# Second expert product by seven products of quarter blocks, in a two-layer attention and mixture-of-experts kernel

## The chip, the core and the metric

One Trainium2 chip, one core. The metric is device time in microseconds (us) of one execution, the median of several runs. Engines are called as in the profile: PE (matrix products), DVE (vector), ACT (scalar, activations), POOL (GpSimd), SP (the queue that issues most plain DMAs). On-chip memory is SBUF, PE writes its results to PSUM.

## The reference, cut to what matters

4096 tokens in all, as 4 x 1024 in layer 0 and 8 blocks of 512 here; width 256. Four stages follow each other, each with a residual and layer norms: a gated attention and a low-rank feed-forward (layer 0), a 16-head attention with relu weights (layer 1), and a mixture of 8 experts with expert choice (layer 1). The change is mostly in the last; its lines:

```python
def _L1_ffn_ref(x, Wg, W1, b1, W2, b2):
    n = b * l                                  # 4096
    k = min(max(int(n * C / e), 1), n)         # 1024 tokens for each of 8 experts
    S = jax.nn.sigmoid(xt @ Wg).T
    G, I = jax.lax.top_k(S, k)
    ex = xt[I]
    hid = gelu(einsum('ekh,ehf->ekf', ex, W1) + b1)              # 256 -> 1024
    out = (einsum('ekf,efh->ekh', hid, W2) + b2) * G[..., None]  # 1024 -> 256
    new_x = zeros_like(xt).at[I.reshape(-1)].add(out.reshape(-1, h))
# then x = x + layernorm(new_x)
```

Each expert takes the 1024 tokens that score highest for it, so a token may be in several experts or in none.

## The kernel before, in words

All products are in float32. Layer 0 takes the first 400 us or so, layer-1 attention the time to about 966 us, the rest is the mixture of experts.

**Layer-1 attention.** Scores, relu and weighted values of 16 heads run as one stream on PE (L1528, L1549), the relu split between ACT (L1705) and DVE (L1707). A planner written out in the kernel, the loop from L1665 on, keeps estimates of when each engine is free. Other work comes as `Part`s, each with its cost per engine, its needs and a condition `when`; `beside` lists those with PE work, `rest` those without. `next_piece` picks a part to put on PE between two groups of scores, `go_on` releases the others. Two limits, MOST and AT_LAST, say how much may be released; AT_LAST holds for the last half block of queries. When a block, a half or (at the end) a quarter of a block is done, `close` (L1291) follows: output projection (`project_tile`, PSUM tile `pt` or, for the last quarter, `pts`), residual y, norms, the rows for the gate (`hg`), its transposes (`tpg`) and the gate product (`pg`). For the last quarter these steps are `at_once` (L1408), written out in order: first half of the projection, the weighted values' last division, `go_on_down_to(1)` (which releases what the earlier quarter still has open), then the second half of the projection.

**Search and lists.** For each expert the threshold of the 1024 best scores is found by steps of compare (L1819), count and a small PE product (L1833). Then the list of its tokens is built (sort, rank, `places` L1960, `collect` L1976) and its rows are gathered by eight indirect DMAs of 128 rows on POOL's queue (`got`, L2000). Expert 0's search and list run ahead; those of the others are steps of an `agenda`, taken by `go_on_with_lists(u, time)` between pieces of expert work.

**Experts.** An expert has 1024 tokens in two halves q of 512 (u = 2e + q), each of 4 chunks of 128 rows. `turn` (L2162) transposes gathered rows on PE and copies them to xT. In experts 0 to 2 and 7, `feed_forward(u)` (L2270) runs the first product, eight blocks of 128 hidden columns by 512 tokens, with gelu on ACT, then `project_back(u)` (L2302), so that each half goes through both products before the next. In experts 3 to 6 the first product covers both halves at once in `feed_forward_by_seven` (L2220): the 2x2 block product is formed by seven products instead of eight (Winograd's form), from sums of weights (`weight_sums`, L2185, four POOL operations of 128x512 for an expert, row L2195) and sums of tokens (`token_sums`, DVE, L2202). Then `project_back` runs twice.

**Second product.** `project_back` takes the chunks one by one: 8 matmuls of 128x256 into a PSUM tile `py` (two buffers), then on DVE bias (L2326) and gate (L2327) into y, then on POOL's queue an indirect DMA that adds the rows of y to `acc_d` in DRAM (L2328, one per chunk). Two scatters of one expert touch different rows, but the build orders each scatter behind the landing of the one before; only for expert 6 (`beside_each_other`) is that taken out. In expert 7 the sums stay in SBUF: `accg` is gathered from `acc_d` after the last scatter of expert 6, the product is added to it (L2322), and statistics, norms and outputs are woven in by the table `beside_last` (`read_back`, `all_stats` L2041, `all_out`, `known` L2087, `chosen_*`). `fetch_last` issues eight gathers of x (`xg`) for it. Weights of expert e + 2 are loaded (`load_expert`, SP, two of 1 MB) at the end of expert e.

[...]

Of the kernel before, what the change touches and what calls it, by code (L numbers as in the profile page):

```python
# [19 lines left out]
P = 128  # L20
D = 256
# [53 lines left out]
def kernel(  # L75
# [1028 lines left out]
    with ExitStack() as st3:  # L1104
# [186 lines left out]
        def close(t, h, oT, tiles, at_end):  # L1291

            y = None

            def new_y():
                nonlocal y
                y = wk.tile([P, NJ, D], F32, tag="y", name="y", bufs=1)
                last_use["y"] = [] if at_end else [parts[5, i] for i in tiles]

# [108 lines left out]
            def at_once(by_weight, back, go_on_down_to):  # L1408
# [8 lines left out]
                    project_tile(pt, i, (0,))  # L1417
                by_weight()
                back()
                go_on_down_to(1)  # L1420
                for i, pt in pts:
                    project_tile(pt, i, (1,))

                idle, psum = (two_banks(name)[:, 0, :] for name in ("idle", "psum"))
                ones = wk.tile([P, P], F32, tag="parts", name="ones")
# [69 lines left out]
            for i in tiles[1::2]:  # L1495
# [8 lines left out]
                        tensor=0.53, scalar=0.59,  # L1504
                    )
                )
            outs[0].when = lambda: done(last_use["y"])
            parts[7, tiles[0]].when = lambda: done(last_use["hg"])
            turns[0].when = may_turn
            gates = Part(gate, [(turns[-1], 1)], tensor=0.65, vector=0.4)  # L1510
# [154 lines left out]
        while True:  # L1665
# [6 lines left out]
                break  # L1672
            at = pe[0]
            Part.now = at / 1.6
            n = max(len(waiting) + len(made) - LAG, 0)
            group_ends, piece = False, None
            if n:
                left = to_end(waiting[0]) + 1
                if left <= n + 1:
                    n, group_ends = left, True  # L1680
                piece = next_piece(1 if not group_ends and left - n <= 2 * STEP else 0)
                if piece is not None and piece.spaced:
                    if since < 1 and len(beside) < MANY:
                        piece = None
                    else:
                        since = -1
                since += 1
            longer = piece.tensor if piece is not None else 0.0
            scored = at + 0.19
            end = scored + 0.22 * len(made) + 0.1 + 0.432 * n + longer  # L1690
            most = MOST if made[0][0][4] == 1 else AT_LAST
            by = end + (0.0 if any(part.ready() and part.takes[1] for part in rest) else 0.5)
            early = 0
            for k, (unit, sc) in enumerate(made):
                scored = max(scored, banks.pop(0)) + 0.22
# [54 lines left out]
    with ExitStack() as st4:  # L1750
# [28 lines left out]

        weights = [load_expert(0), load_expert(1)]  # L1780

        each = keep.tile([P, P, NTILE], BF16, name="each")
        behind_exp = mybir.DependencyInfo(mybir.DependencyClass.Sync, mybir.DependencyReason.DATA)
        whole = nc.scalar.activation(each, count_p.unsqueeze(2).to_broadcast([P, P, NTILE]), AF.Copy, scale=-1.0 / P)
        tc.add_manual_dep(whole.ins, state["exp"].ins.name, behind_exp, reason="the last scores go ahead")

        whole_c = keep.tile([P, NC], F32, name="whole_c")
# [93 lines left out]
        def in_stored(half):  # L1881

            room = xs[ADDED - 1].rearrange("p j d -> p (j d)")[:, half * TB : (half + 1) * TB]
            return room.bitcast(BF16).rearrange("p (a b) -> p a b", b=QT)

        class List:

# [72 lines left out]
            def places(self, part):  # L1960
                js = slice(part * QT, (part + 1) * QT)
                if part < 2:
                    self.at[part] = wk.tile([P, P, QT], BF16, tag="at", name="at", bufs=2)
                else:
                    self.at[part] = in_stored(part - 2)
                nc.vector.tensor_tensor(
                    self.at[part],
                    self.lo[:, js].unsqueeze(1).to_broadcast([P, P, QT]),
                    each[:, :, js],
                    ALU.is_equal,  # L1970
                )

            def collect(self, part):
                for j in range(part * QT, (part + 1) * QT):
                    u = 32 * (j % 4)
                    nc.tensor.matmul(  # L1976
                        parts[u : u + 2 * NC, 0:P],
                        lhsT=self.pair[:, j, :, :].rearrange("p v c -> p (v c)"),
                        rhs=self.at[part][:, :, j - part * QT],
                        start=(j < 4),  # L1980
                        stop=(j >= NTILE - 4),
                    )
                if part == 3:
                    self.listed = wk.tile([P, P], BF16, tag="listed", name="listed")
                    nc.scalar.copy(self.listed, parts[:, 0:P])
# [173 lines left out]
        QPE = NC // NJ  # L2159
        xT = {}  # L2160

        def turn(u, c, half=None):  # L2162

            if c == 0 and not half:
                xT[u] = wk.tile([P, DC, TB], F32, tag="xT", name="xT")
            e, q = divmod(u, QPE)
            tiles = range(NJ) if half is None else range(half * NJ // 2, (half + 1) * NJ // 2)
            tp = ps.tile([P, NJ, P], F32, tag="mm", name="tp", bufs=5)
            for i in tiles:
                nc.tensor.transpose(tp[:, i, :], lists[e].got[q * NJ + i][:, c * P : (c + 1) * P], ident)  # L2170
                if u == 0 and c == 0 and i == 0:

                    keep_busy(first, 4)
            cols = slice(tiles[0] * P, (tiles[-1] + 1) * P)
            copy = nc.scalar.copy if by_seven(e) else nc.vector.tensor_copy
            copy(xT[u][:, c, cols], tp.rearrange("p j t -> p (j t)")[:, cols])  # L2176

        def by_seven(e):
# [25 lines left out]
        def turns_within(u):  # L2204

            e, q = divmod(u, QPE)
            if u == QPE * NE - 1:
                return {}
            turns = {c: (lambda c=c: turn(u + 1, c)) for c in range(DC)}
            if q == QPE - 1 and by_seven(e + 1):  # L2210
                both = [
                    turns[0], turns[1], lambda: turn(u + 2, 0), lambda: token_sums(e + 1, 0), lambda: turn(u + 2, 1),
                    *(lambda n=n: token_sums(e + 1, n) for n in (1, 2, 3)),
                ]
                return {0: both[0:1], 1: both[1:4], 2: both[4:]}
            if by_seven(e) and q == 0:
                return {}
            return {2: [turns[0], turns[1]]} if u == 1 else {1: [turns[0]], 2: [turns[1]]}

        def feed_forward_by_seven(e):  # L2220
# [18 lines left out]
            for f in range(HC):  # L2239
# [19 lines left out]
                product(d, s4, b22, False, True, f)  # L2259
                nc.vector.tensor_tensor(c12, u2, d, ALU.add)  # L2260
                gelu(1, f, c12)
                go_on_with_lists(QPE * e, 3.0)
            for q in range(QPE):
                if q == 0 and by_seven(e + 1):
                    weight_sums(e + 1, gelus[-1])
                if q == 0 and e == NE - 2:
                    fetch_last()
                project_back(QPE * e + q, hid[q])

        def feed_forward(u):  # L2270
            e, q = divmod(u, QPE)
            w1, w2 = weights[e]
            hid = wk.tile([P, FC, TB], F32, tag="hid", name="hid")

            n = TB if u else TB // 2
            for h in range(TB // n):
# [3 lines left out]
                for f in range(FC):  # L2280
# [13 lines left out]
                    )  # L2294
                    if u or h or f not in (FC - 5, FC - 4, FC - 3):
                        go_on_with_lists(u, 1.75 if u else 0.87)
                    aside(u, "f", f)
            if q == QPE - 1 and by_seven(e + 1):
                weight_sums(e + 1, gelu)
            project_back(u, hid)  # L2300

        def project_back(u, hid):  # L2302

# [2 lines left out]
            ahead = turns_within(u)  # L2306
            for i in range(NJ):
                k = q * NJ + i
                py = ps.tile([P, D], F32, tag="y", name="py")
                for f in range(FC):  # L2310
                    nc.tensor.matmul(  # L2311
                        py,
                        lhsT=hid[:, f, i * P : (i + 1) * P],
                        rhs=w2[:, f, :],
                        start=(f == 0),
                        stop=(f == FC - 1),
                    )
                for do in ahead.get(i, ()):
                    do()
                gates = lists[e].got[k][:, D + e : D + e + 1]  # L2320
                if e == NE - 1:
                    nc.vector.scalar_tensor_tensor(accg[:, k, :], py, gates, accg[:, k, :], ALU.mult, ALU.add)  # L2322
                    aside(u, "i", i)
                    continue
                y = wk.tile([P, D], F32, tag="y", name="y", bufs=7)
                nc.vector.tensor_tensor(y, py, mb2[:, e, :], ALU.add)  # L2326
                nc.vector.tensor_scalar(y, y, gates, None, ALU.mult)  # L2327
                scatter = nc.gpsimd.indirect_dma_start(  # L2328
                    out=acc_d[:, :],
                    out_offset=lists[e].at_chunk(k),  # L2330
                    in_=y,
                    in_offset=None,
                    bounds_check=NT - 1,
                    oob_is_err=True,
                    compute_op=ALU.add,
                )
                if e == NE - 2:

                    beside_each_other(scatter, summed)
                go_on_with_lists(u, 3.4 if by_seven(e) else 2.3)  # L2340

# [85 lines left out]
```

## Time and profile before

| what | us |
|---|---|
| median of 3 runs | 1468.24 (1467.99 to 1468.54) |
| profiled execution: its own time | 1469.22 |
| its span, first to last instruction | 1467.0 |
| PE busy | 1414.9 |
| DVE, ACT, POOL busy | 869.4, 738.2, 530.3 |

The profile shows one execution; busy times are sums over the span, and an average over stages with different limits. Expert 0 begins at about 994 us, expert 1 at 1055, expert 2 at 1117, experts 3 to 6 at 1178, 1234, 1290 and 1346, expert 7 at 1401. The costliest groups of the experts' stage: second product L2311 (1024 records, 228.6 us), first product L2285 (288 records, 114.8 us), scatters L2328 (56, 88.5 us), gathers L2000. The profile has two records for each matmul instruction of these float32 products. A row of a group reads: line, engine, operation, output and inputs with shapes, count, then busy time and the mean ns of one (which overlap on PE, so that mean times count is more than busy), then idle time before it and what ended it. A row of a time line reads: start, length, engine, line, operation, and in brackets the idle time before it with what ended it. A row of the table by stretches has the stretch, its length, busy time and count for PE, PE's weight loads (PEld), DVE, ACT and POOL, the granted PE clock as a share, the share of DMA engines busy, and GB/s.

### The profile page before, as it was taken

The page shows a single profiled execution, that of the slowest core. Times are in us where ns is not written, and L with a number is a line of the kernel's source. Part 1 is how long each engine was busy: PE and PEld are TensorE (multiplying, and loading weights), DVE is VectorE, ACT ScalarE, POOL GpSimd, SP SyncE. Part 2 cuts the span into 40 slices and gives each one's busy share as a digit, 9 for nine tenths or more (in the row PEclk, how much of TensorE's full clock was granted, in tenths as well). Part 3 has the DMA queues.
Part 4 walks back from the last instruction along what each step waited for, and adds up shares of the span by engine and source line. Part 5 has one row for each costly group of instructions (what it writes and reads, how often), then busy time and mean ns, then how long its engine had stood idle before and what let it go on. Part 6 is the DMA issues. An engine that isn't in the chain of part 4 may idle for free. (4 is left out here: it accounts for less than half of the span.)

```text
span 1467.0 us, 26441 instructions
## 1 busy us (share of the span) xinstructions
PE 1414.9 (96%) x10392; PEld 859.9 (59%) x10392; DVE 869.4 (59%) x2134; ACT 738.2 (50%) x1013; POOL 530.3 (36%) x662
## 2 busy tenths in 40 slices
PE   8999999999899999999999999849999999999997
PEld 4666666667544545544554447617666657757674
DVE  5457655566554637574766587785545766364346
ACT  4244454443368887887878788522221131231243
POOL 4123232223352314333334223413425325543655
PEclk9999999999999999999999999969999999999999
DMA  8400000001642373448145611151414223343364
GB/s 223 139 1 1 1 1 1 1 1 59 209 143 88 115 232 101 138 137 240 55 140 170 191 59 31 45 162 39 104 22 126 49 76 69 80 100 60 78 168 133
DMA packets 104853, 138.76 MB, mean 95 GB/s; under 512 B 25469, under 2 KB 64794, under 8 KB 104602
## 3 DMA queue, kind: packets, MB, share of 16 engines
q1 hardware_dynamic: 74512, 81.75, 17.9%
q0 software_dynamic: 30160, 55.32, 15.8%
q8 instruction: 81, 1.33, 0.4%
q14 instruction: 42, 0.34, 0.1%
q10 hardware_dynamic: 58, 0.01, 0.0%
HBM read 75.29 MB, written 61.51 MB: 93 GB/s over the span
## 5 line engine op out<-in xcount | busy, mean ns | idle before, releaser
L1705 ACT ACTIVATE w<-sc 128x1024 f32<-128x1024 f32 x394 | 378.9, 1024 | 61.4 <-PE sc L1528 60.9
L1549 PE MATMUL po<-w,vaug 128*17 128x256 f32 (+1 forms) x4608 | 255.9, 358 | 1.0 <-DVE turned L1607 0.6
L2311 PE MATMUL py<-w,hid 128*128 128x256 f32 x1024 | 228.6, 380 | 0.0
L2311 PEld LDWEIGHTS py<-w,hid 128*128 128x128 f32 x1024 | 191.9, 190 | 29.6 <-issue 4.2
L1707 DVE TENSOR_SCALAR w<-sc 128x1024 f32<-128x1024 f32 x118 | 143.7, 1221 | 79.1 <-PE sc L1528 76.0
L1549 PEld LDWEIGHTS po<-w,vaug 128*17 128x17 f32 x4608 | 116.4, 97 | 117.3 <-issue 48.4
L1528 PE MATMUL sc<-q,kT 64*128 64x512 f32 (+1 forms) x1152 | 170.8, 404 | 2.9 <-ACT w L1705 1.5
L2328 POOL DMA_INDIRECT acc_d<-y,idx x56 | 88.5, 1579 | 164.6 <-issue 36.4
L1528 PEld LDWEIGHTS sc<-q,kT 64*128 64x128 f32 x1152 | 90.0, 184 | 84.1 <-issue 45.5
L2292 ACT ACTIVATE hid<-ph,mb 128x512 f32<-128x512 f32 (+1 forms) x72 | 46.0, 638 | 159.3 <-PE ph L2285 133.4
L2285 PE MATMUL ph<-xT,w 128*128 128x512 f32 (+1 forms) x288 | 114.8, 552 | 0.3 <-DVE xT L2176 0.3
L2000 POOL DMA_INDIRECT got<-tok_d,idx x64 | 66.3, 1036 | 76.3 <-DVE idx L1990 34.1
L2285 PEld LDWEIGHTS ph<-xT,w 128*128 128x128 f32 x288 | 52.6, 190 | 52.1 <-issue 49.1
L371 POOL DMA_DIRECT2D kT<-k_d x32 | 23.4, 732 | 117.9 <-PE sc L1528 54.3
L722 PE MATMUL pg<-nT,wh 128*128 128x512 f32 x128 | 61.4, 612 | 1.5 <-ACT nT L661 1.5
L2326 DVE TENSOR_TENSOR y<-py,mb 128x256 f32<-128x256 f32 x56 | 23.5, 420 | 65.8 <-PE py L2311 53.7
L848 PE MATMUL py<-wo,oT 128*128 128x256 f32 x256 | 61.6, 384 | 0.0
L738 PE MATMUL pv<-wh,nT 128*128 128x512 f32 x128 | 59.7, 592 | 0.0
L848 PEld LDWEIGHTS py<-wo,oT 128*128 128x128 f32 x256 | 47.5, 190 | 17.6 <-issue 11.1
L746 ACT ACTIVATE v<-v 128x512 f32<-128x512 f32 x32 | 20.2, 630 | 62.7 <-DVE v L745 62.7
L586 POOL TENSOR_TENSOR x<-x,y 128x1024 f32<-128x1024 f32 x13 | 30.6, 2355 | 56.3 <-ACT y L575 56.3
L1137 POOL TENSOR_TENSOR rsb<-veb,mhalf 128x1 f32<-128x1 f32 x30 | 19.7, 657 | 83.9 <-DVE veb L1136 83.9
(345 smaller groups left out, 2355.2 us busy)
## 6 DMA issues: line engine op xcount, KB each, us to landing
q<-q_d POOLq DMA_DIRECT2D x16, 1024.0 KB, 6.0
kT<-k_d POOLq DMA_DIRECT2D x32, 512.0 KB, 8.4
w<-in_L_ffn_W_dram SPq DMA_DIRECT2D x16, 1024.0 KB
k_d<-parts SPq DMA_DIRECT2D x48, 256.0 KB
q_d<-parts SPq DMA_DIRECT2D x48, 256.0 KB
acc_d<-logits SPq DMA_DIRECT2D x8, 512.0 KB
tok_d<-hg SPq DMA_DIRECT2D x30, 128.0 KB
x<-in_L_attn_x_dram SPq DMA_DIRECT2D x7, 512.0 KB
```

The source lines that it names most:

```text
L722: nc.tensor.matmul(pg, lhsT=wh[:, c, HID + e * P : HID + (e + 1) * P], rhs=d["nT"][:, c, :], start=(c == 0), stop=(c == DC - 1),)
L738: nc.tensor.matmul(pv, lhsT=d["nT"][:, c, i * P : (i + 1) * P], rhs=wh[:, c, 0:HID], start=(c == 0), stop=(c == DC - 1),)
L848: nc.tensor.matmul(py, lhsT=d["oT"][:, e, :], rhs=wo[:, e, :], start=(e == 0), stop=(e == EC - 1))
L1528: nc.tensor.matmul(sc[:, j, m * n : (m + 1) * n], lhsT=row["kT"][t, r][rows, u, (kt + m) * P : (kt + m + 1) * P], rhs=row["q"][qh, t][rows ...
L1549: nc.tensor.matmul(po[rows : rows + HD + 1, at : at + n], lhsT=row["v"][:, kt + m, HQ * t + 4 * r + 2 * u + j, :], rhs=w[:, j, (2 * m + pa ...
L1705: nc.scalar.activation(w, sc, AF.Relu)
L1707: nc.vector.tensor_scalar(w, sc, 0.0, None, ALU.max)
L2000: return nc.gpsimd.indirect_dma_start(out=dst, out_offset=None, in_=rows[:, :], in_offset=self.at_chunk(c), bounds_check=NT - 1, oob_is_er ...
L2285: nc.tensor.matmul(ph, lhsT=w1[:, c, f * P : (f + 1) * P], rhs=xT[u][:, c, h * n : (h + 1) * n], start=(c == 0), stop=(c == DC - 1),)
L2292: gelu = nc.scalar.activation(hid[:, f, h * n : (h + 1) * n], ph, AF.Gelu, bias=mb1[:, e * FC + f : e * FC + f + 1])
L2311: nc.tensor.matmul(py, lhsT=hid[:, f, i * P : (i + 1) * P], rhs=w2[:, f, :], start=(f == 0), stop=(f == FC - 1),)
L2328: scatter = nc.gpsimd.indirect_dma_start(out=acc_d[:, :], out_offset=lists[e].at_chunk(k), in_=y, in_offset=None, bounds_check=NT - 1, oob ...
```

## The change

- The second product of experts 0 to 6 is formed by seven products over both halves (`project_back_by_seven`): blocks are halves of tokens by halves of hidden columns, and halves of W2's columns. Its matmuls are 128x128. The sums of W2 (`back_sums`) are four POOL operations of 128x512, put behind the expert's first gelu (of the second half in experts 0 to 2); the sums of hidden values are four DVE operations of 128x2048; further DVE operations join the products; the bias is laid down by ACT with the gate as its scale, and DVE adds gate times product to it.
- The order on PE is p1, p4, the rest of p1, p7, p6, p5, the rest of p5, with the next expert's turns between. p4 takes the fourth sum of W2.
- All eight scatters come late: four after p5 (chunks 4 to 7), four after its rest (chunks 0 to 3), before one per chunk. y has nine buffers instead of seven.
- Experts 0 to 2: both halves go through the first product, with the second half's turns inside the first half's, and only then the second product. The turns' PSUM tiles are of tag "y", the copies of experts 1 and 2 go to ACT.
- Attention's end: the quarter before the last has its own buffer for y, `go_on_down_to(1)` comes behind the second half of the projection, and the planner is freer to put parts in while the last half block is scored.
- `each` and the tables of places have four token blocks to an inner run, `each` 128x512 instead of 128x4096.
- Expert 7 keeps `project_back`.

The core of the diff:

```diff
@@ close
+            quarter = len(tiles) < NJ and not at_end
             def new_y():
                 nonlocal y
+                if quarter:
+                    y = wk.tile([P, NJ, D], F32, tag="parts", name="y_parts")
+                    return
@@ at_once
-                go_on_down_to(1)
                 for i, pt in pts:
                     project_tile(pt, i, (1,))
+                go_on_down_to(1)
...
-            outs[0].when = lambda: done(last_use["y"])
+            outs[0].when = lambda: quarter or done(last_use["y"])
@@ planner
+            most = MOST if made[0][0][4] == 1 else AT_LAST
-                piece = next_piece(1 if not group_ends and left - n <= 2 * STEP else 0)
+                piece = next_piece(1 if most is MOST and not group_ends and left - n <= 2 * STEP else 0)
-            most = MOST if made[0][0][4] == 1 else AT_LAST
-            by = end + (0.0 if any(part.ready() and part.takes[1] for part in rest) else 0.5)
+            waits = most is MOST and any(part.ready() and part.takes[1] for part in rest)
+            by = end + (0.0 if waits else 0.5)
@@ lists
-        each = keep.tile([P, P, NTILE], BF16, name="each")
+        each = keep.tile([P, P, 4], BF16, name="each")
@@ turn
-            copy = nc.scalar.copy if by_seven(e) else nc.vector.tensor_copy
+            copy = nc.scalar.copy if 0 < e < NE - 1 else nc.vector.tensor_copy
@@ feed_forward_by_seven
+                if f == 0:
+                    back_sums(e, gelus[-1])
                 go_on_with_lists(QPE * e, 3.0)
-            for q in range(QPE):
-                if q == 0 and by_seven(e + 1):
-                    weight_sums(e + 1, gelus[-1])
-                if q == 0 and e == NE - 2:
-                    fetch_last()
-                project_back(QPE * e + q, hid[q])
+            if by_seven(e + 1):
+                weight_sums(e + 1, gelus[-1])
+            if e == NE - 2:
+                fetch_last()
+            project_back_by_seven(e, hid)
@@ new functions
+        def back_sums(e, behind):
+            (b11, b12), (b21, b22) = back_blocks(e)
+            t1, t2, t4 = (room.rearrange("p (f n) -> p f n", n=P) for room in back_rooms[:3])
+            for dst, x, y in ((t1, b12, b11), (t2, b22, t1), (b12, b22, b12), (t4, b21, t2)):
+                after_all(nc.gpsimd.tensor_tensor(dst, x, y, ALU.subtract), [behind])
...
+            def product(bank, a, b, start, stop):
+                for i in range(NJ):
+                    if i == NJ // 2:
+                        lists_too(0)
+                    for f in range(HC):
+                        nc.tensor.matmul(bank[:, i * P : (i + 1) * P], lhsT=a[:, f, i * P : (i + 1) * P],
+                            rhs=b[:, f, :], start=start and not i and not f, stop=stop and f == HC - 1,
+                            skip_group_check=True)
+            def of_bias(q):
+                for k in range(q * NJ, (q + 1) * NJ):
+                    ys[k] = wk.tile([P, D], F32, tag="y", name="y", bufs=9)
+                    nc.scalar.activation(ys[k], mb2[:, e, :], AF.Identity, scale=gates[k])
+            def add(q, n, src):
+                for i in range(NJ):
+                    k = q * NJ + i
+                    y = ys[k][:, n * P : (n + 1) * P]
+                    nc.vector.scalar_tensor_tensor(y, src[:, i * P : (i + 1) * P], gates[k], y, ALU.mult, ALU.add)
...
+            p1 = new_bank("p1")
+            product(p1, a11, b11, True, True)
+            nc.scalar.copy(u2, p1)
+            nc.vector.tensor_tensor(s1, a21, a22, plus)
+            nc.vector.tensor_tensor(s3, a11, a21, sub)
+            lists_too(1)
+            p4 = new_bank("p4")
+            product(p4, a22, t4, True, True)
+            nc.vector.tensor_tensor(s2, s1, a11, sub)
+            lists_too(1)
+            product(p1, a12, b21, False, True)
+            of_bias(0)
+            add(0, 0, p1)
+            nc.vector.tensor_tensor(s4, a12, s2, sub)
...
+            product(p7, s3, t3, True, True)
...
+            product(p6, s2, t2, True, True)
+            nc.vector.tensor_tensor(u2, u2, p6, plus)
+            of_bias(1)
+            nc.vector.tensor_tensor(v, u2, p7, plus)
+            nc.vector.tensor_tensor(c21, v, p4, plus)
...
+            product(p5, s1, t1, True, True)
+            add(1, 0, c21)
+            nc.vector.tensor_tensor(v, v, p5, plus)
...
+            add(1, 1, v)
+            put(1)
+            product(p5, s4, b22, False, True)
+            nc.vector.tensor_tensor(u2, u2, p5, plus)
+            add(0, 1, u2)
+            put(0)
@@ feed_forward
+                    if e < NE - 1 and not q and h == TB // n - 1 and f in (FC - 5, FC - 2):
+                        turn(u + 1, int(f == FC - 2), tag="y")
+                    if e < NE - 1 and q and not f:
+                        back_sums(e, gelu)
...
-            project_back(u, hid)
+            if e == NE - 1:
+                project_back(u, hid)
+            elif q == QPE - 1:
+                project_back_by_seven(e, [hids[k] for k in range(QPE)])
```

`put(q)` issues the indirect DMAs of four chunks as L2328 did. `lists_too` calls `go_on_with_lists` with 1.2 us, between products in all experts and in the middle of each product in experts 0 to 2.

## The prediction, made before the change was run

> **What bounds the kernel now.** First the page's busy shares and slices: who is full, and where.
>
> ```profile
> PE 1414.9 (96%) x10392; PEld 859.9 (59%) x10392; DVE 869.4 (59%) x2134; ACT 738.2 (50%) x1013; POOL 530.3 (36%) x662
> PE   8999999999899999999999999849999999999997
> PEclk9999999999999999999999999969999999999999
> ```
>
> PE is full except in slices 26 and 27 (about 950 to 1030 us: end of layer-1 attention, search). Then stretch by stage over the experts (columns: busy PE, PEld, DVE, ACT, POOL, clock, DMA, GB/s):
>
> ```profile
> 942.00:966.00 24.00, 14.62 (x63) 7.29 (x63) 15.29 (x51) 4.88 (x12) 7.50 (x21) 0.86 0.46 164
> 994.20:1055.20 61.00, 60.67 (x290) 45.22 (x291) 31.36 (x104) 13.33 (x25) 22.77 (x19) 1.00 0.26 60
> 1116.80:1178.40 61.60, 61.24 (x260) 40.28 (x256) 42.08 (x102) 13.50 (x21) 26.73 (x20) 1.00 0.31 69
> 1234.30:1290.20 55.90, 55.90 (x236) 37.33 (x236) 27.62 (x61) 15.53 (x25) 27.29 (x22) 1.00 0.36 79
> 1435.00:1467.00 32.00, 22.16 (x84) 15.58 (x82) 18.56 (x56) 8.48 (x16) 15.61 (x18) 0.91 0.41 115
> ```
>
> Rows two to four are experts 0, 2 and 4: PE has no gap to give, so a PE saving there counts in full until another engine is late. GpSimd looks idle at 27 of 56 us. It isn't: the time line of its scatters in expert 4 shows a fixed beat.
>
> ```profile
> 1271.36 1.62 POOL L2328 DMA_INDIRECT acc_d<-y,idx  x1 [0.16 <-issue]
> 1275.96 1.56 POOL L2328 DMA_INDIRECT acc_d<-y,idx  x1 [2.98 <-DVE y L2327]
> 1280.43 1.55 POOL L2328 DMA_INDIRECT acc_d<-y,idx  x1 [2.91 <-issue]
> 1284.90 1.54 POOL L2328 DMA_INDIRECT acc_d<-y,idx  x1 [2.92 <-DVE y L2327]
> ```
>
> 1.55 us of work, then 2.9 us of waiting for the last scatter to land, with all behind it on POOL's queue waiting too: 4.5 us each, 36 us for an expert's eight, in a queue that the page calls 36% busy.
>
> **What the change saves.** (1) Second product of experts 0 to 6. The group of L2311 has 1024 records in 228.6 us, so 0.223 us each; an expert has 64 matmuls of 128x256 in 128 records, 28.6 us. By seven it is 7 x 16 = 112 matmuls 128 wide, 224 records. The nearest row at that width is layer 0's:
>
> ```profile
> 146.52 0.39 PE L824 MATMUL po<-head,kv 128*128 128x128 f32 x2
> 146.74 0.39 PE L820 MATMUL po<-packed,v 128*128 128x128 f32 x2
> 146.97 0.39 PE L824 MATMUL po<-head,kv 128*128 128x128 f32 x2
> L824 PEld LDWEIGHTS po<-head,kv 128*128 128x128 f32 x224 | 34.0, 192 | 0.0
> ```
>
> Two records start every 0.223 us, 0.1115 each, although each has a weight load recorded at 192 ns; so loads overlap and don't set the pace. 224 x 0.1115 = 25.0 us, 3.6 less per expert, 25.1 less for seven. Were loads to set it (192 ns), it would be 43 us and +100 in all; the row excludes nearly all of that, and I take 25.0.
>
> (2) End of layer-1 attention. On PE's time line the first half of the last output product is done at 942.9, the second runs only at 950.95 to 952.85, behind gate transposes that wait 3.59 and 1.20 us for GpSimd. The change puts the second half at once behind the first, and moves the quarter before last's gates into the score loop: about 7.7 us earlier, less the 1.4 us of PE work moved into a loop that is full (905 to 942: PE 36.5 of 37). I take -6.5, between -3 (gates needed then anyway) and -8. The clock rule of the skill bears here (TensorE: Matmul & The Clock Gate, Part 1): after about 3.4 us idle PE runs at half clock until it has been busy as long. The trace agrees: those records take 0.53 us after the gap and 0.22 elsewhere, and the stretch was granted 0.86. So each stall that I find below costs about 2 us more than its length; a sum without it would be about 5 lower.
>
> (3) Gone besides: 16 vector operations per expert (0.42 and 0.45), beside PE. Smaller tables of places and `each`: same element count on the vector engine, nothing on the path; an estimate of -0.5 to +0.5.
>
> Savings: -31.6.
>
> **What it costs.** New vector work per expert: 4 sums of 128x2048, about 2.2 us each (from 0.69 at 512 wide, L2202, less its fixed part), 16 scaled adds (0.28 each; 256 wide took 0.48 in L2322), 5 of 512 (0.69): 16.7 us within 25 us of PE. On ACT eight bias activations and a copy, 4 us, hidden at 15 of 56. The rest depends on POOL's queue, whose order in the changed kernel its build tells. Per expert it gets four sums (1.27 to 1.32 us each, row L2195; 5.3 us), of which the fourth (t4) is needed by p4, PE's second product of the seven; and all eight scatters now come together, at the expert's end. They hide only while POOL is done with the last expert's scatters before p4. Expert by expert, times from its start:
>
> Expert 0: the second product also holds six search steps of about 1.95 us: 16.7 + 11.7 = 28.4 on the vector engine for 25.0 on PE. +3.5, and +1 in the first product. Bounds 2 to 7.
>
> Expert 1: its sums stand behind all eight scatters of expert 0. First at -1, last at -1 + 7 x 4.55 = 30.9, issued by 32.4, sums to 37.7. The first product with its turns takes about 31.2 (61.6 less 28.6 and the turns that leave), p1 3.6: p4 wants t4 at 34.8. Stall 3 at least. Here a rule speaks against the change (SBUF — State Buffer, Who interferes with whom): a vector operation with two SBUF inputs and a GpSimd one that reads SBUF lock each other out for a whole instruction. The row, in expert 2 of before:
>
> ```profile
> 1159.78 1.30 DVE L1819 TENSOR_TENSOR ge<-by_e,tried 128x224 bf16<-128x224 f32 x4
> 1163.32 4.52 DVE L1819 TENSOR_TENSOR ge<-by_e,tried 128x224 bf16<-128x224 f32 x4
> 1163.38 1.45 POOL L2195 TENSOR_TENSOR x<-w 128x512 f32<-128x512 f32 x1 [10.16 <-ACT hid L2292]
> ```
>
> The same four compares took 4.52 us beside POOL's sums, 1.30 alone. In the changed kernel s1 and s3 (2.2 each, two SBUF inputs) fall just where the late sums run, so t4 is ready at about 41.7: stall 7. By the row of POOL's sums alone 3, by the rule 7; I take 7 plus 2 of cold clock: +9 (3 to 11).
>
> Expert 2: its sums are behind eight scatters of expert 1 and eight gathers (1.32 apart): sums start 35.4, t4 at 40.6 to 42, p4 wants it at 33.1. Stall 8.5; the next weight sums then hold the vector engine's search steps, +3; cold clock 2: +13.5 (8 to 17).
>
> Experts 3 to 6: p4 is later there (30.0) and t4 earlier (22.7), since fewer scatters go ahead: nothing. Expert 3's gathers (of 4) are late: +2 (0 to 4).
>
> Tail. In before the last scatter of expert 6 is issued 1.1 us after expert 7's start and landed by 6; the accumulators are read back and the chain goes on:
>
> ```profile
> 1402.31 1.55 POOL L2328 DMA_INDIRECT acc_d<-y,idx  x1 [1.32 <-DVE y L2327]
> 1409.46 1.41 DVE L2041 BATCH_NORM_STATS2 stc<-back_w 128x6 f32<-128x256 f32 x4 [7.42 <-DMA back_w<-acc_d]
> 1418.41 0.48 DVE L2322 SCALAR_TENSOR_TENSOR accg<-py,got,accg 128x256 f32<-128x256 f32 x1 [2.39 <-PE py L2311]
> ```
>
> The first accumulation at 1418.41 still waited 2.39 for PE, so the cover is small. After, eight scatters follow one another 1.85 apart, landing about 16 after the start instead of 6; statistics at 19.5 instead of 8.3, first accumulation at 26 instead of 17.2. Two PSUM buffers: PE's third group (20.9) waits 5 to 5.7, cold clock 2. It goes straight to the end: +7.5 (5 to 9.5).
>
> Costs: 4.5 + 9 + 13.5 + 2 + 7.5 = 36.5. Net -31.6 + 36.5 = +5 on the profiled 1469.22 (span 1467.0 and 2.2 around it), that is 1474; the median of the runs lies 1.0 below it, so 1473.
>
> **Rivals.** (A) PE stays the bound and faster wins: POOL's scatters keep closer than 4.55 us (as expert 6's do, 1.85), so t4 is there before p4 in experts 1 and 2 and the tail keeps its cover. It decides at about 33 to 35 us from the expert's start. Then only +4.5, +2, and perhaps 3 of the tail stay: -31.6 + 9.5 = -22, 1446. Against it: the same scatters to the same accumulator wait in every expert of before but 6.
> (B) The slower side by one mechanism, in full: POOL's queue, priced at expert 1 +11, expert 2 +17, tail +9.5 beside 4.5 + 2 = 44, giving +12.5: 1481. It decides when t4 is ready over 7 us behind p4's turn. This is my case at its upper end; the beat of 5.2 to 6.8 us, seen where a weight load is issued beside scatters, would bring it.
> (C) Loads bound the 128-wide products: +101 in place of -25 on the forecast: about 1599. The dense row speaks against it.
> (D) It does not do what it says at the attention's end (another wait takes its place): 6.5 more; or stalls overlap with what follows and are 5 smaller: about 1468.
>
> **How the numbers follow.** POOL bound as forecast, 1473 to 1480: 0.42; in full, above: 0.17; C: 0.02; balance, within 0.2%: 0.15; A and what lies between it and balance: 0.24. A measurement of this kernel can tell 0.2% (2.9 us) from no change. The likeliest time is 1473. The range: 1455 leaves out the lower half of A, 1484 the top of B and C. Faster 0.24, same 0.15, slower 0.61. The forecast's own case alone spans 1468 to 1481.
>
> **What would show it.** Right: records of p1's group 0.11 us apart; a PE wait of 5 us and more for POOL ahead of p4 in experts 1 and 2, none in 4 to 6; expert 4's stretch near 52.5 instead of 55.9; a wait of PE for the vector engine in expert 7 at some 20 us from its start; the vector engine's first output sum 1.5 us behind the last score. Wrong: scatters of one expert closer than 4.5 us; no PE gap over 2 us between experts 0 and 3; weight loads 190 ns apart.

## The result and the profile after

The changed kernel takes 1505.7 us (median of 4 runs, 1503.3 to 1506.86), the kernel before 1468.39 (4 runs); ratio 1.0251, 95% interval 1.0234 to 1.0269. It is 37 us slower, where 5 were forecast. The profiled execution of the changed kernel took 1503.3 us, with a span of 1501.5.

First the page of the changed kernel: busy shares, and PE and its clock in 40 slices.

```profile
PE 1404.5 (94%) x11064; PEld 877.2 (58%) x11064; DVE 941.8 (63%) x2188; ACT 767.4 (51%) x1085; POOL 599.8 (40%) x690
PE   8999999999899999999999999499987999898977
PEclk9999999999999999999999999799998999999989
```

PE is busy for 10 us less although the span is 34 longer: it now has gaps all through the experts, and some slices are at a lower clock. Next, who PE waited for from 985 us on, the four largest (columns: total us, times, longest).

```profile
PE p L2320 <- POOL wv L2290: 17.0, 2, 10.6
PE py L2449 <- DVE accg L2459: 9.6, 1, 9.6
PE p L2320 <- DVE x L2387: 9.0, 7, 2.3
PE tp L2175 <- DMA got<-tok_d,idx: 7.1, 7, 2.2
```

`wv` is t4; L2387 adds p5 to v, L2459 adds a product to expert 7's sums. Before the change PE's waits from 995 us on were 0.7 us in all:

```profile
PE parts L1833 <- DVE counts L1826: 0.4, 1, 0.4
PE ph L2285 <- DVE xT L2176: 0.3, 1, 0.3
```

The stages, from the first product of one expert to that of the next (the forecast's own terms added up beside them):

| stage | before | after | change | forecast |
|---|---|---|---|---|
| up to expert 0's first product | 995.1 | 988.1 | -7.0 | -6.5 |
| expert 0 | 61.5 | 63.6 | +2.1 | +0.9 |
| expert 1 | 62.0 | 66.9 | +4.9 | +5.4 |
| expert 2 | 59.6 | 72.9 | +13.3 | +9.9 |
| expert 3 | 55.9 | 59.7 | +3.8 | -1.6 |
| expert 4 | 56.0 | 60.3 | +4.3 | -3.6 |
| expert 5 | 56.0 | 58.9 | +2.9 | -3.6 |
| expert 6 | 55.0 | 52.4 | -2.6 | -3.6 |
| expert 7 to the end | 66.0 | 78.8 | +12.8 | +7.5 |

The changes add up to the two spans' difference, 34.5, but for rounding. Of the 30 us that the forecast missed, 20 lie in experts 3 to 5 and 5 in the tail.

The saving on PE itself came as worked out. PE's time line of the changed kernel in expert 3, and in expert 1 behind a wait:

```profile
1216.86 3.73 PE L2320 MATMUL p<-w,hid 128*128 128x128 f32 x32
1220.43 3.74 PE L2320 MATMUL p<-wv,hid 128*128 128x128 f32 x32
...
1092.10 5.61 PE L2320 MATMUL p<-wv,hid 128*128 128x128 f32 x32 [6.39 <-POOL wv L2290]
```

A product starts 3.57 us behind the one before, so 0.1115 us a record and 25.0 us for seven; expert 6, where PE is idle for only 0.6 us, is 2.6 us shorter. Behind a wait of 6.39 the same 32 records took 5.61. That is the cold clock (the granted clock was 0.50 from 1092.10 to 1095.84), 1.9 us, as forecast.

Now GpSimd's queue over one expert (changed kernel, from expert 3's first scatter to expert 4's; the lines left out are scatters, gathers and sums):

```profile
1248.66 1.63 POOL L2342 DMA_INDIRECT acc_d<-y,idx  x1 [5.65 <-DVE y L2338]
1253.41 2.46 POOL L2342 DMA_INDIRECT acc_d<-y,idx  x1 [3.13 <-DVE y L2338]
...
1288.44 1.61 POOL L2342 DMA_INDIRECT acc_d<-y,idx  x1 [0.30 <-PE p L2320]
...
1296.71 1.01 POOL L2005 DMA_INDIRECT got<-tok_d,idx  x1 [0.30 <-issue]
...
1308.94 1.61 POOL L2342 DMA_INDIRECT acc_d<-y,idx  x1 [5.65 <-DVE y L2338]
```

From the first scatter of one expert to the first of the next it is 60.3 us, as long as the expert: 49.1 to the end of the issue of its last gather (1297.7), 1.8 until the last transpose that needs these rows starts (1299.55), and 9.4 until the next y is made; the queue itself waits for that y in the last 5.65. It is a loop: scatters, gathers, turns, product, scatters. PE has work for some 52 us of it, as expert 6 shows. What PE sees of it at the loop's end:

```profile
1294.24 0.33 PE L2175 MATMUL tp<-ident,got 128*128 128x128 f32 x1 [2.23 <-DMA got<-tok_d,idx]
1299.55 0.33 PE L2175 MATMUL tp<-ident,got 128*128 128x128 f32 x1 [0.44 <-DMA got<-tok_d,idx]
...
1306.14 5.47 PE L2320 MATMUL p<-w,hid 128*128 128x128 f32 x32 [2.25 <-DVE x L2387]
```

Waits of 2.23, 0.44 and 2.25, and 1.7 of cold clock behind the last one (5.47 for 3.74): 6.6 of the 7.9 us by which expert 4 is longer than expert 6. This is the gap that the forecast put at nothing.

### The profile page after: what moved, and what is told of

Its sections match the earlier page's. It is cut to its first block, busy times and chain, and to the rows that moved or that the text cites. A ratio compares the mean times of both kernels' runs of the same rounds, so it can differ in the third digit from the quotient of the medians.

```text
span 1501.5 us, 28024 instructions
## 1 busy us (share of the span) xinstructions
PE 1404.5 (94%) x11064; PEld 877.2 (58%) x11064; DVE 941.8 (63%) x2188; ACT 767.4 (51%) x1085; POOL 599.8 (40%) x690
## 5 line engine op out<-in xcount | busy, mean ns | idle before, releaser
L1710 ACT ACTIVATE w<-sc 128x1024 f32<-128x1024 f32 x395 | 379.9, 1023 | 60.7 <-PE sc L1532 60.2
L2342 POOL DMA_INDIRECT acc_d<-y,idx x56 | 94.8, 1693 | 161.3 <-DVE y L2338 51.2
L2320 PE MATMUL p<-w,hid 128*128 128x128 f32 x896 | 110.5, 285 | 9.0 <-DVE x L2387 9.0
L2320 PEld LDWEIGHTS p<-w,hid 128*128 128x128 f32 x896 | 107.5, 200 | 13.5 <-DVE x L2387 10.6
L2005 POOL DMA_INDIRECT got<-tok_d,idx x64 | 88.0, 1374 | 52.6 <-DVE idx L1995 33.8
L2181 ACT COPY xT<-tp 128x512 f32<-128x512 f32 x24 | 13.8, 584 | 104.9 <-PE tp L2175 104.9
L722 PE MATMUL pg<-nT,wh 128*128 128x512 f32 x128 | 61.1, 609 | 1.5 <-ACT nT L661 1.5
L738 PE MATMUL pv<-wh,nT 128*128 128x512 f32 x128 | 59.7, 592 | 0.0
L1137 POOL TENSOR_TENSOR rsb<-veb,mhalf 128x1 f32<-128x1 f32 x30 | 19.5, 649 | 86.8 <-DVE veb L1136 86.8
```

The lines of the kernel that those rows point to most:

```text
L722: nc.tensor.matmul(pg, lhsT=wh[:, c, HID + e * P : HID + (e + 1) * P], rhs=d["nT"][:, c, :], start=(c == 0), stop=(c == DC - 1),)
L738: nc.tensor.matmul(pv, lhsT=d["nT"][:, c, i * P : (i + 1) * P], rhs=wh[:, c, 0:HID], start=(c == 0), stop=(c == DC - 1),)
L1710: nc.scalar.activation(w, sc, AF.Relu)
L2005: return nc.gpsimd.indirect_dma_start(out=dst, out_offset=None, in_=rows[:, :], in_offset=self.at_chunk(c), bounds_check=NT - 1, oob_is_er ...
L2320: nc.tensor.matmul(bank[:, i * P : (i + 1) * P], lhsT=a[:, f, i * P : (i + 1) * P], rhs=b[:, f, :], start=start and not i and not f, stop= ...
L2342: scatter = nc.gpsimd.indirect_dma_start(out=acc_d[:, :], out_offset=lists[e].at_chunk(k), in_=ys[k], in_offset=None, bounds_check=NT - 1, ...
```

## The experiments

Each time is beside the kernel before on the same chip, where its median was 1467.23 (runs 1 to 4), 1470.72 (5 to 7 and 11) or 1468.39 us (8 to 10 and 12). Differences to the changed kernel are to its 1505.7 (ratio 1.0251, 1.0234 to 1.0269), measured beside a before of 1468.39; as they cross chips, one of about 3 us or less is not read as a difference.

**1. Attention's end alone.** In the kernel before, only the hunks of `close`, `at_once` and the planner:

```diff
                 back()
-                go_on_down_to(1)
                 for i, pt in pts:
                     project_tile(pt, i, (1,))
+                go_on_down_to(1)
...
```

> The kernel before with the change to the end of layer-1 attention alone. Theory 1 (the second half of the last output product no longer stands behind the gate transposes that wait for GpSimd): 7 us faster than before, 1461, with the search's first small product 7 us earlier and the experts' stage as before. Rival (the released work comes back as another wait): within 2 us of before.

1461.0 us against 1467.23, ratio 0.9958 (0.9943 to 0.9974). The term holds: -6.2, forecast -6.5. In its profile expert 0 starts at 986.5 us, in that of the changed kernel at 988.1, so the smaller tables of places, which only the latter has, show no gain there.

**2. Scatters side by side.**

```diff
-                    if e == NE - 2:
-                        beside_each_other(scatter, summed)
+                    beside_each_other(scatter, summed if e == NE - 2 else puts[e])
+                    after_all(scatter, puts[e - 1] if e else [])
...
+        puts = [[] for _ in range(NE)]
```

> The changed kernel, but scatters of one expert don't wait for each other's landing (each still waits for those of the expert before). Theory 1 (the beat of 4.5 us on GpSimd's queue makes t4 late in experts 1 and 2 and the gathers late in 3 to 5): PE's waits for wv, 17 us, go, with some 4 us of cold clock, and the waits for gathered rows, 8 us; part of the tail, 4: 30 us faster than the changed kernel, about 1475. Rival A (t4 is late because GpSimd's sums and the vector engine's two-input sums lock each other out): half of the waits for wv stay, about 1493. Rival B (landings one by one are the limit and waiting moves from the queue to the DMA): no change, 1505.

1474.09 us, ratio to before 1.0053 (1.0034 to 1.0071), so some 30 faster than the changed kernel, as theory 1 had it. Its scatters of expert 4 follow each other less than 2 us apart, and before the first GpSimd's queue has waited 14.09 us for y, where it was 5.65 in the changed kernel:

```profile
1291.20 1.62 POOL L2342 DMA_INDIRECT acc_d<-y,idx  x1 [14.09 <-DVE y L2338]
1293.13 1.67 POOL L2342 DMA_INDIRECT acc_d<-y,idx  x1 [0.30 <-DVE wop L2394]
1295.10 1.67 POOL L2342 DMA_INDIRECT acc_d<-y,idx  x1 [0.30 <-issue]
```

The waits for `wv` are gone (17.0 to 0) and those for gathered rows nearly (7.1 to 0.3). Experts 3 to 5 take 53.8, 54.4 and 54.4. The beat is the cause, and rivals A and B fall as the main one. But expert 2 took 74.0, no less than with the wait: something else stood behind it (run 9).

**3. The operation that frees p5 first.** In `project_back_by_seven`:

```diff
-            lists_too(1)
             p5 = new_bank("p5")
             product(p5, s1, t1, True, True)
-            add(1, 0, c21)
             nc.vector.tensor_tensor(v, v, p5, plus)
+            lists_too(1)
+            add(1, 0, c21)
```

> The changed kernel, but the vector operation that reads p5's first half comes ahead of the list step and of the scaled adds. Theory 1 (in experts 3 to 5 the rest of p5 waits for it behind a list step and a token sum on the vector engine's queue, 2.25 us each, and then runs cold, 1.7 us): 12 us faster than the changed kernel, 1494. Rival (what is put behind comes due next: the following expert's first product waits for the token sums): 0 to 4 us faster.

1512.74 us, ratio 1.0327 (1.0299 to 1.0354): 7 slower than the changed kernel. Both expectations missed. The waits for L2387 did go, with their cold clock. But experts 3 to 5 take 58.3, 61.1 and 59.8, since the rows still come when GpSimd's queue brings them. Expert 0 ended 2.7 us earlier, and expert 1 then waited 13.3 us for t4 instead of 6.4: two of the scatters ahead of its sums were followed by the next only after 7.05 and 7.76 us, in the changed kernel 4.6 on average. Both of these steps begin within half a microsecond of the issue of a 1 MB weight load (1049.38 and 1079.90); that the load delayed the landing, as rival B reads it in the kernel before, is likely, but wasn't tried apart. Expert 1 is 8 us longer than in the changed kernel, about the whole loss. So the gain ahead of the queue was not passed on, and the loss may be one of timing.

**4. Gathers of x later.** `fetch_last` taken out of expert 6, the gathers issued by `beside_last` in expert 7:

```diff
-            if e == NE - 2:
-                fetch_last()
...
-            (0, "i", 3): [(all_out, 3), (all_scaled, 4), (all_stats, 5)],
+            (0, "i", 3): [(all_out, 3), (all_scaled, 4), (all_stats, 5), (fetch_x, 0, 1, 2, 3)],
```

> The changed kernel, but the eight gathers of x for the last expert are issued in the last expert instead of ahead of expert 6's scatters. Theory 1 (expert 6's scatters, all at its end, stand behind them on GpSimd's queue, and the last expert's accumulators are late by that): scatters start 7 us earlier, PE's wait of 9.6 us for the accumulation shrinks to 2 or 3 and its cold clock goes with it: 8 us faster, about 1497. Rival (the bunching alone sets it, the queue would be late anyway, or the gathers now delay the outputs): under 3 us.

1507.09 us, ratio 1.0271 (1.0254 to 1.0289): no difference to the changed kernel, so the rival was right. PE's wait for the accumulation fell from 9.6 to 3.65 us, near what theory 1 had. But the gathers now stood ahead of the powers of GpSimd that the output's scaling on ACT waits for, gelu stood behind that scaling on ACT, and PE waited 5.23 for gelu. The wait moved along the same queue.

**5. Seven in experts 3 to 6 alone.** Experts 0 to 2 as before, chunk by chunk.

```diff
+        def per_chunk(e):
+            return e in (0, 1, 2) or e == NE - 1
...
-            if e == NE - 1:
+            if per_chunk(e):
                 project_back(u, hid)
```

> The changed kernel, with the second product of experts 0 to 2 as before the change (chunk by chunk, each half through both products); experts 3 to 6 stay by seven. Theory 1, made sharper (in experts 3 to 5 GpSimd's queue itself is full: eight scatters of 4.5 us, eight gathers of 1.3 to 2, eight sums of 1.3 are 58 us and more, whatever precedes): experts 0 to 2 fall back to 61 us each, experts 3 to 5 stay near 60, the tail stays long: 1483 to 1487. Rival (experts 3 to 5 are late only because the experts ahead of them were): they fall to 53, the tail to 69, about 1455.

1486.52 us, ratio 1.0104 (1.0078 to 1.0129). Experts 0 to 2 are near their old times, experts 3 to 5 take 60.8, 61.2 and 61.1. The tail takes 77.7. All is as theory 1 had it: experts 3 to 5 aren't late because of what precedes them, GpSimd's queue is full there by itself.

**6. Sums ahead of the scatters.**

```diff
-            add(1, 0, c21)
+            behind = add(1, 0, c21)
+            ahead_sums = back_sums(e + 1, behind) if e + 1 < NE - 1 else []
...
+                    after_all(scatter, ahead_sums)
...
```

> The changed kernel, but the sums of W2 for expert e + 1 stand on GpSimd's queue ahead of expert e's scatters, not behind them. Theory 1 (the queue's whole time for an expert is the bound, so an order only says who is late): the waits for wv go in experts 1 and 2 (17 us and 4 of cold clock), but expert 2 shows the search waits of some 10 us that the run with scatters side by side has too, and in 3 to 5 scatters and gathers come 5 us later: their 60 us stay or grow. 1488 to 1500. Rival (only the place of the sums is wrong): 1478 or below, with experts 3 to 5 near 57.

1511.46 us, ratio 1.0262 (1.0229 to 1.0295). No wait for `wv` is left, and yet it is no faster than the changed kernel (by ratio some 2 us slower, within the spread): expert 1 gains 6.5, expert 2 keeps 72.1, experts 3 to 6 take 60.2, 63.6, 63.1 and 60.8, in all 16 us more than in the changed kernel. The stages go the way of theory 1, but its time, 1488 to 1500, was missed: it had the growth in experts 4 to 6 and the tail too small. What was put first on the full queue made the rest later.

**7. Scatters side by side in the kernel before.** The edit of run 2 in `project_back`.

> The kernel before, with scatters of one expert not waiting for each other's landing. Theory 1 (there the beat is hidden, since each chunk's scatter has 3.5 us of PE work of its own beside it and the queue's total of 52 is under PE's 56): 1467, within 2 us of before. Rival (the beat costs something there already): 3 us or more faster.

1472.01 us against 1470.72, ratio 1.0006 (0.9994 to 1.0018). No difference: experts 0 to 5 have the times of the kernel before, within 0.2 us each, so there the beat cost nothing until the change took away what hid it. Expert 6, whose scatters were side by side already, took 61.4 us in this profile instead of 55.0: PE waited 3.22 us for the vector engine's step from py to y, which had itself waited 7.68, and ran cold. The trace does not name what that step waited for, and it wasn't tried.

**8. p4's wait kept warm.**

```diff
+            if e in (1, 2):
+                keep_busy(ps.tile([P, TB], F32, tag="mm", name="idle", bufs=5), (26, 44)[e - 1])
             p4 = new_bank("p4")
```

> The changed kernel, with 26 (expert 1) and 44 (expert 2) idle bf16 products of 0.215 us put on PE between p1 and p4, where it waits for t4. If the cold clock after such a wait costs its own 1.8 us each time, p4 runs at 0.11 us a record in both and the kernel is 3.6 us faster than the changed one, about 1502, as long as GpSimd's queue doesn't take the gain back; if that queue is the bound there, p4 is warm but what is won shows as a longer wait further on, and the time is within 2 us of 1505.7.

PE's time line of this kernel in expert 1:

```profile
1083.09 5.78 PE L203 MATMUL idle<-all_b 128*128 128x512 bf16 x26
1090.03 3.84 PE L2320 MATMUL p<-wv,hid 128*128 128x128 f32 x32 [1.17 <-POOL wv L2290]
```

p4 is warm, 3.84 us instead of 5.61. Expert 1 is 1.4 us shorter and expert 2 0.7. From expert 0's start to expert 7's it is 433.4 us instead of 434.6: the waits behind grew. As a whole the run took 1512.35 us, ratio 1.0295 (1.0275 to 1.0314), 6.6 more than the changed kernel, so neither expectation was met, and more than all of it lies in expert 7, where PE waited 11.4 us for the accumulation and then 5.25 for gelu, which stood behind ACT's waits for GpSimd, as in run 4. Why that wait comes up in some of these kernels and not in others wasn't tried.

**9. Sums of expert 2 left out**, with scatters side by side. The kernel leaves out `back_sums(2)` and `weight_sums(3)`, so that experts 2 and 3 don't form what they should.

```diff
         def back_sums(e, behind):
+            if e == 2:
+                return
...
```

> The changed kernel with scatters of one expert side by side, and GpSimd's sums of W2 for expert 2 and of W1 for expert 3 left out (eight operations of 128x512; the output of these experts is then not the reference's). Expert 2 took 74.1 us with scatters side by side, with no wait for t4. Theory (GpSimd's sums and the vector engine's compares and list operations with two SBUF inputs lock each other out, and PE's search products, in order, wait): expert 2 at 63 to 66, 8 to 11 us faster than the run with scatters side by side. Rival (the vector engine is simply full in expert 2's second product): 71 or more.

1460.43 us, ratio to before 0.9939 (0.9923 to 0.9956), some 14 faster than run 2, where 8 to 11 were expected. Expert 2 falls from 74.0 to 61.3, so the rival falls. What those eight operations of some 1.3 us each did there can be read in run 2's time lines, first the vector engine and GpSimd, then PE:

```profile
1134.49 4.53 DVE L1824 TENSOR_TENSOR ge<-by_e,tried 128x224 bf16<-128x224 f32 x4
...
1135.70 1.41 POOL L2290 TENSOR_TENSOR w<-w 128x512 f32<-128x512 f32 x1
1137.07 1.41 POOL L2290 TENSOR_TENSOR wv<-w,wk 128x512 f32<-128x512 f32 x1
...
1140.20 0.19 PE L1838 MATMUL parts<-counts,all_b 128*128 128x32 bf16 x1 [4.66 <-DVE counts L1831]
1140.23 6.74 PE L2417 MATMUL ph<-xT,w 128*128 128x512 f32 x8
```

Four compares of 1.30 us in all took 4.53 beside the sums. PE's small search product waits 4.66 for them. The first product stands behind it on PE, starts 0.03 us later and runs cold: 6.74 us for what takes 3.68 (the granted clock was 0.50 from 1139.56 to 1146.38). This agrees with the rule of the Trainium skill (SBUF — State Buffer, Who interferes with whom) that a vector operation with two SBUF inputs and a GpSimd one that reads SBUF hold each other up. In the other direction as well: in expert 1 of the changed kernel POOL's third and fourth sum took 3.31 us each beside the vector engine's s1 and s3.

**10. Expert 6 chunk by chunk**, with scatters side by side.

```diff
+            if per_chunk(e):
+                for q in range(QPE):
+                    project_back(QPE * e + q, hid[q])
+                return
             project_back_by_seven(e, hid)
...
```

> The changed kernel with scatters of one expert side by side and expert 6's second product chunk by chunk as before. With all eight scatters at its end the last expert and what follows took 74.4 us in the run with scatters side by side, before the change 65.8. Theory (the bunched scatters land late and the accumulators with them): 66 to 67 there, expert 6 back at 55 to 58, so 3 to 6 us faster than that run, about 1469. Rival (the tail is late for another reason): 74 stays, 1477.

1466.98 us, ratio 0.9986 (0.9977 to 0.9994), 7 faster than run 2. Expert 7 and what follows take 66.2 us instead of 74.4, expert 6 54.4 instead of 52.4. The bunched scatters are 8 of the tail's 12.8 us; the other 4.4 had gone with the beat in run 2 (78.8 to 74.4).

**11 and 12. Versions put together.** Run 11: scatters side by side, seven in experts 3 to 5, with the edit of run 3. Run 12: scatters side by side, seven in experts 1, 3, 4 and 5, and in expert 6

```diff
                 for q in range(QPE):
                     project_back(QPE * e + q, hid[q])
+                    if e == NE - 2 and q == 0:
+                        fetch_last()
```

> A version put together from the findings: the changed kernel with scatters of one expert side by side, the second product by seven in experts 3 to 5 alone (0 to 2 and 6 chunk by chunk as before), and the operation that reads p5 ahead of the list step. Theory 1: attention's end 6.5 us faster, experts 3 to 5 at 53 instead of 56, the rest as before: 1453. Rival (in experts 3 to 5 the vector engine's queue takes GpSimd's place): they stay at 55 or more, 1459 to 1461.

> A version put together: scatters of one expert side by side, the second product by seven in experts 1, 3, 4 and 5, chunk by chunk in 0, 2 and 6, the gathers of x between the halves of expert 6. By the stages of the runs so far: 61.5 + 59.0 + 61.6 + 54.0 + 54.4 + 54.3 + 55.0 + 66 and attention's end: 1453. Rival (the locks of GpSimd and the vector engine strike elsewhere): experts 2 or 3 are 4 us longer, 1458 or more.

Run 11: 1460.28 us, ratio 0.9921 (0.9894 to 0.9949), so the rival was nearer: experts 4 and 5 at 54.5, but expert 3 at 59.6, where list operations on the vector engine met GpSimd's sums (PE waited 3.68), and expert 6 at 58.1. Run 12: 1453.26 us, ratio 0.9894 (0.9878 to 0.9911). It is the fastest of all, 15 us below the kernel before, of which 6 are attention's end. That the sum of 1453 came out is in part luck: expert 3 took 60.2 instead of 54.0, as the rival had it (PE waited 3.67 beside GpSimd's sums), the tail 68.0 instead of 66, and other experts were shorter than assumed. The profiled execution, 1457.68, was also the slowest of the four. Nearly 6 us are left in expert 3.

## Why the prediction was wrong

**Right.** PE's pace at 128 columns (0.1115, measured the same), so 3.6 us saved per expert: expert 6 shows 2.6 of it net (PE busy 3.2 less, and 0.6 idle). Attention's end (-6.5, measured -6.2 alone). Expert 1: t4 ready at 40.4 us from its start, 41.7 forecast; stall 6.4 (7 forecast), cold clock 1.9 (2). That the sign is slower and that GpSimd's queue is why. Two readings were off without moving the sum: the slices with gaps run from 917 to 990 us, not 950 to 1030, and the cold records behind attention's gap start 0.43 us apart, not 0.53.

**The step that failed** is "Experts 3 to 6: p4 is later there (30.0) and t4 earlier (22.7), since fewer scatters go ahead: nothing." It asked only whether t4 is in time. It is, but the gathers of the next expert stand on the same queue, and the forecast never summed the queue over a whole expert. From the forecast's own numbers: eight scatters of 4.55, eight gathers of 1.32, eight sums of 1.3 are 36.4 + 10.6 + 10.4 = 57.4 us. Before the change there were four sums, 52.2 us, under PE's 56. The change added 5.2 us to the queue and took PE's 56 down to 52.4, so the queue became the longer one. That sum alone gives +5 per expert against the forecast; measured were 5.4, 7.9 and 6.5 in experts 3 to 5. The rest is in part that the queue's operations grew (gathers from 1.0 to as much as 2.6 us, in expert 4 by 2.8 in all) and that the loop closes through PE and the vector engine; it wasn't taken apart further. Runs 2 and 5 show it: without the beat 54, with the beat 61 whatever precedes. Run 7 shows that the beat without the change cost experts 3 to 5 nothing. No run left the new sums out with the beat kept, so their 5.2 us are a sum of times from the traces.

**The tail** had the right mechanism and too small a size: stall 9.6 instead of 5 to 5.7. The forecast took the scatters to land 16 us after expert 7's start. As the queue was late by the beats of expert 5, expert 6's first scatter was issued 3.6 us after expert 7's start (in run 2, without the beat, 2.1 ahead of it, and there PE waited 4.4), the last one at 1439.3, 16.6 after the start, and the first statistics came at 23.7 instead of 19.5. The lines of the changed kernel that answer to those shown of before:

```profile
1439.34 1.54 POOL L2342 DMA_INDIRECT acc_d<-y,idx  x1 [0.30 <-issue]
1446.39 1.41 DVE L2046 BATCH_NORM_STATS2 stc<-back_w 128x6 f32<-128x256 f32 x4 [21.58 <-DMA back_w<-acc_d]
1453.57 5.72 PE L2449 MATMUL py<-w,hid 128*128 128x256 f32 x16 [9.59 <-DVE accg L2459]
```

**Expert 2** was too low by 3.4, and its terms did not add as forecast. The wait for t4 was there (10.6, 8.5 forecast), but taking it away gave nothing back (run 2: 74.0). In the changed kernel GpSimd's eight sums run while PE waits for t4 and just behind (1156.4 to 1167.2), and the search and list steps cost PE some 2 us; without that wait the same sums cost 12.7 (run 2 against run 9), where the forecast had 3. So the two waits covered each other, and their costs can't be added. This is read from the two runs; none left the sums out with the beat kept.

**The rivals.** A (GpSimd's scatters closer, 1446) described the remedy, not the change: with the beat gone the time was 1474, because of expert 2 and the tail. B, the queue priced in full, had the right sign and mechanism, but was priced at t4 and the tail only. C fell. D's first half fell (run 1).

## What to carry to other kernels

Sum each in-order queue over one period of the loop, waits for landings included, and hold it against the bound engine's period, before and after: a queue that is 40% busy can be full. Once the faster engine had fallen below that sum, none of the reorderings tried here helped (on the queue runs 4 and 6, on the vector engine run 3), nor a warm clock (run 8); shortening the queue's chain did (run 2). Forming the sums on another engine wasn't tried. A stall that is removed uncovers the next one, so price a stage with each wait left out in turn.

## What the runs showed of the hardware

A gap on PE of 2.25 us was enough for the half clock: the 32 records behind it took 5.47 us instead of 3.74, in experts 3, 4 and 5 alike. In expert 4, where the gap ended at 1306.14, the table by stretches of the changed kernel reads:

```profile
1304.05:1307.46 3.41, 1.32 (x11) 1.32 (x12) 3.41 (x9) 0.46 (x1) 0.00 (x0) 1.00 0.00 0
1307.46:1310.87 3.41, 3.41 (x18) 3.41 (x17) 1.48 (x5) 0.00 (x0) 1.61 (x1) 0.50 0.00 0
1310.87:1314.28 3.41, 3.41 (x14) 1.91 (x13) 2.60 (x7) 0.58 (x1) 0.61 (x1) 1.00 0.68 140
```

The granted clock fell to 0.50 only 1.3 us after PE had work again, and came back 3.41 us later, which makes the 1.7 us lost. The Trainium skill (TensorE: Matmul & The Clock Gate, Part 1) puts the gap that does this at about 3.4 us; here the measurement decides. A wait of 2.23 for gathered rows, ahead of p6 in expert 4, left the clock as it was, so a gap of this length may or may not do it.

GpSimd's issue of a gather took 1.0 us alone and up to 2.8 while the vector engine ran sums with two SBUF inputs. In expert 3 of the changed kernel:

```profile
1229.02 2.28 DVE L2368 TENSOR_TENSOR hid<-hid 128x2048 f32<-128x2048 f32 x1
1229.61 2.57 POOL L2005 DMA_INDIRECT got<-tok_d,idx  x1 [0.30 <-issue]
```
